# A state-space convolution with a mixture of experts on one core: x copied to the output ahead, the shared expert's sums added by transfers, and three stages in one written order

## The chip, the core and the metric

The kernel runs on one core of one Trainium2 chip. The metric is device time in microseconds (us) of one launch. TensorE (PE) does the matrix products, VectorE (DVE), ScalarE (ACT) and GpSimd (POOL) the elementwise work; transfers (DMA) are issued from the queues of SyncE (SP), ACT and POOL. Each engine works through its own instructions in their order and waits on semaphores for the others.

## The reference

```python
# x: [128, 32, 512], itok: [128] lengths
K = 2 * Re(sum_n Ct[h, n] * exp(dtA[h, n] * l))         # one kernel of 512 taps for each of 32 heads
y = causal_convolution(x, K) + x * D[:, None]           # along the 512 positions
y = y * (arange(512) < itok[:, None, None])             # cut to each row's length
t = y.reshape(4096, 512)                                # tokens
scores = sigmoid(t @ gate_w.T) + bias                   # 16 experts
w, idx = top_k(scores, 4);  w = w / sum(w)
out = sum over the 4 chosen experts of  w * (silu(t @ Wg.T) * (t @ Wu.T)) @ Wd.T
out = out + (silu(t @ Sg.T) * (t @ Su.T)) @ Sd.T        # the shared expert
return x + out.reshape(x.shape)
```

All of it is in float32. The inner size of an expert is 256.

## The kernel before

The work has three stages.

**Convolution** (loop at L831 over `NB` = 8 blocks of `HB` = 4 heads). For each head, `convolve` multiplies x (transposed on the host, `xt`) with a strip of shifted kernels (L520), masks by length into `yb` (L527, DVE), turns it with TensorE into the order by length (L530), and ACT copies it into `yT` (L531), which stays in SBUF (inside the tile `store`). Two buffers each hold `xt` and `strip`, so the loads of the next block (L151, L419, SP's queue) start at a block's start. The block's `yb` goes to the HBM buffer `y_rows` from ACT's queue (L841). `gates` then makes the gate scores of the block: partial products `parts` (L549), a copy `by_head` (L557, ACT), and sums over the quarters into `pg` (L560). After every second block `route` works out sigmoid, the best 4 of 16 and the weights `cw` on DVE (L582 to L615), turns `cw` back into row order on TensorE (`cw_ps`, L618), copies it (L620, ACT) and stores it beside the rows of `y_rows` (L621, SP).

**Shared expert** (`unit_step`, L953). The tokens are cut into `NU` = 8 units of 512. For a unit, `up` makes gate and up products (L904, `p_g` and `p_u`, each for two halves `it` of the inner size; between 1 and 4 row tiles are used, by the longest row in the unit), ACT applies Silu (L963), DVE multiplies (L966, tile `z`), and `down` makes four products of 128 tokens for the unit before (L930, two PSUM buffers `o`). The rows of x belonging to those tokens have been fetched by an indirect transfer from POOL's queue (`fetch`, L918, six buffers `xg`); DVE adds x to the product (L937), and an indirect transfer on POOL's queue puts the rows into `out` (L939). Between these pieces `next(making)` runs the next piece of the generator `slots` (L629): it counts tokens for each expert, places them in tiles of 128 slots, and builds the lists `get` and `put` with 128 pairs of one-hot matrices (L793, L794 on DVE; L782 on PE, eight in a step). The experts' weights are loaded into a ring of 8 places as their places come free (L980).

**Routed experts** (L1102 onward). For each tile of 128 slots: gather rows of `y_rows` (L869, POOL), transpose (L1012), gate and up products (L1044), Silu, multiplication with the weight, transpose (L1062), down product (L1070), copy (L1079, DVE) and an indirect transfer that adds the rows to `out` (L1080). Its output buffers are the first three of `xg`. `order` (L1092) makes SP wait for all adds so far where a new expert starts, and a tile's add waits for SP's mark.

Order: the convolution stage with `gates` and `route` is ordered by a scheduler. The units and the routed tiles are each written within `tc.manual_schedule(engines=None)` (L982 and L1102), with the rest of `making` in between. In the build, unit 0's first two up products stand ahead of the last block's `parts`, sums and `cw_ps` on PE, and the first routed transposes stand inside unit 7.

Of the kernel before, what the change touches and what calls it, by code (L numbers as in the profile page):

```python
# [31 lines left out]
I32 = mybir.dt.int32  # L32
# [43 lines left out]
def ssm_moe_kernel(  # L76
# [68 lines left out]
    y_rows = d1.tile([B * H, YW], F32, tag="y_rows", name="y_rows")  # L145
    y_bh = y_rows.rearrange("(b h) w -> b h w", h=H)
    x_rows = x.rearrange("b h l -> (b h) l")
# [117 lines left out]
    def exp_into(dst, v, name):  # L265
        shape = list(v.shape)
        k, q = (ks1.tile(shape, F32, tag=f"exp_{t}", name=f"{name}_{t}") for t in "kq")
        s = ks1.tile(shape, I32, tag="exp_s", name=f"{name}_s")
        exp_parts(v, q, k, s)
        nc.vector.scalar_tensor_tensor(dst, q, 1.0, s.bitcast(F32), ALU.add, ALU.mult)  # L270
# [10 lines left out]
    exp_into(dn.rearrange("p a c -> p (a c)"), logs.rearrange("p a c -> p (a c)"), "dn")  # L281
# [233 lines left out]
    def convolve(tb, q, xt, yb):  # L515
        h = tb * HB + q
        py = ps_g.tile([P, L], F32, tag="g", name=f"py{h}")
        for jt in range(KT):

            nc.tensor.matmul(  # L520
                py[:, : L - jt * P],
                lhsT=xt[:, jt, q, :],
                rhs=strip[tb][:, q, jt * P :],
                start=(jt == 0),
                stop=(jt == KT - 1),
            )
        nc.vector.tensor_mul(yb[:, q, :L], py, within)  # L527
        pt = ps_u.tile([P, KT, P], F32, tag="u", name=f"pt{h}")
        for kt in range(KT):
            nc.tensor.transpose(pt[:, kt, :], yb[:, q, kt * P : (kt + 1) * P], to_rank)  # L530
        nc.scalar.copy(  # L531
            yT[:, :, :, h, :].rearrange("p u k b -> p k u b"),
            pt.rearrange("p k (u b) -> p k u b", u=NU),
        )
# [5 lines left out]
    pgs = {}  # L540

    def gates(tb):


        if tb % RB == 0:
            pgs[tb // RB] = ps_o.tile([P, 512], F32, tag="o", name=f"pg{tb}")
        parts = ps_m.tile([P, NU, HB, UB], F32, tag="m", name=f"parts{tb}")
        for kt in range(KT):
            nc.tensor.matmul(  # L549
                parts[kt * QC : (kt + 1) * QC],  # L550
                lhsT=gw[:, kt, :],
                rhs=yT[:, :, kt, tb * HB : (tb + 1) * HB, :],
                start=True,
                stop=True,
            )
        by_head = yp.tile([P, HB, NU, UB], F32, tag="by_head", name=f"by_head{tb}")
        nc.scalar.copy(by_head.rearrange("p h u b -> p u h b"), parts)  # L557
        for q in range(HB):
            n = (tb * HB + q) % (RB * HB)
            nc.tensor.matmul(  # L560
                pgs[tb // RB][:, n * E : (n + 1) * E],
                lhsT=by_head[:, q].rearrange("p u b -> p (u b)"),
                rhs=gather_q,
                start=True,
                stop=True,
            )

    def route(rb):
# [14 lines left out]
        exp_into(neg, neg, f"sig{rb}")  # L583
# [31 lines left out]
        nc.vector.tensor_mul(cw, s, over_e(free))  # L615

        cw_ps = ps_m.tile([P, nh * E], F32, tag="m", name=f"cw_ps{rb}")
        nc.tensor.matmul(cw_ps, lhsT=to_row, rhs=flat(cw), start=True, stop=True)  # L618
        cw_o = stile("cw_o")
        nc.scalar.copy(flat(cw_o), cw_ps)  # L620
        nc.sync.dma_start(out=y_bh[:, hs, L:], in_=cw_o)  # L621
# [203 lines left out]


    xb = load_xt(0)
    nc.sync.dma_start(out=w_sh, in_=w_all[E])

    chunk_at = {0: CHUNKS[1], 2: CHUNKS[2], HB + 1: CHUNKS[3]}  # L830
    for tb in range(NB):  # L831
        yb = yp.tile([P, HB, L], F32, tag="yb", name=f"yb{tb}")
        x_next = load_xt(tb + 1) if tb + 1 < NB else None
        for q in range(HB):
            convolve(tb, q, xb, yb)
            if tb * HB + q in chunk_at:
                c0, n = chunk_at[tb * HB + q]
                kernels(c0, n, *waves(c0, n, 0)[0])
            if q == 0 and tb + 1 < NB:
                kernel_strip(tb + 1)  # L840
        nc.scalar.dma_start(out=y_bh[:, tb * HB : (tb + 1) * HB, :L], in_=yb)  # L841
        gates(tb)
        if tb % RB == RB - 1:
            route(tb // RB)
        xb = x_next
# [4 lines left out]

    def dep(of, on, why):
        tc.add_manual_dep(of.ins, on.ins.name, SYNC, reason=why)
# [40 lines left out]
    xg = homes(fp, "xg", [P, L], 6)  # L893
# [20 lines left out]
    def rows_of(u, q):  # L914
        return bass.IndirectOffsetOnAxis(ap=unit_rows[:, u, q : q + 1], axis=0)

    def fetch(u, q):
        nc.gpsimd.indirect_dma_start(  # L918
            out=at(xg, u * (TU // P) + q),
            out_offset=None,  # L920
            in_=x_rows,
            in_offset=rows_of(u, q),
        )

    def down(u, q):
        n = u * (TU // P) + q
        po, xq = at(p_o, n), at(xg, n)
        for it in range(IT):
# [8 lines left out]
        nc.vector.tensor_add(xq, po, xq)  # L937
        nc.gpsimd.nop()
        put = nc.gpsimd.indirect_dma_start(  # L939
            out=out, out_offset=rows_of(u, q), in_=xq, in_offset=None  # L940
        )
        for other in adds:
            tc.declare_no_dep(put.ins, other.ins, reason="other rows")
        adds.append(put)
# [8 lines left out]
    def unit_step(u):  # L953
# [3 lines left out]
        if u < NU:  # L957
            fetch(u, 0)
            fetch(u, 1)
            k_us[u] = nc.tensor.value_load(k_u[0:1, u : u + 1], min_val=1, max_val=KT)  # L960
            for it in range(IT):
                up(u, it, p_g, 0)
                nc.scalar.activation(sgu[it], p_g[it], AF.Silu)  # L963
                next(making, None)
                up(u, it, p_u, I)
                nc.vector.tensor_mul(at(zu, u)[:, it, :], sgu[it], p_u[it])  # L966
                next(making, None)
        if u > 0:
            for q in range(TU // P):
                down(u - 1, q)  # L970
        if u < NU:
            fetch(u, 2)
            fetch(u, 3)
# [7 lines left out]

    with tc.manual_schedule(engines=None):  # L982
        for u in range(NU + 1):
            unit_step(u)
    for _ in making:
        pass
    put, texp, woff, load, loff, lexp, ntk, fresh, full = (
        made[t] for t in "put texp woff load loff lexp ntk fresh full".split()
    )
# [10 lines left out]
    obs = xg[:3]  # L1000
# [5 lines left out]
    def tokens(t):  # L1006
# [9 lines left out]
        else:  # L1016
# [5 lines left out]
            texp[:, t : t + 1],  # L1022
# [11 lines left out]
    def registers(t):  # L1034
        w0s[t] = nc.tensor.value_load(
            woff[0:1, t : t + 1], min_val=0, max_val=(R - 1) * WSZ
        )
        k_ts[t] = nc.tensor.value_load(ntk[0:1, t : t + 1], min_val=1, max_val=KT)
# [28 lines left out]
    def outer(t):  # L1067
        po = at(p_o, t)
        for it in range(IT):
# [12 lines left out]
            out_offset=bass.IndirectOffsetOnAxis(ap=put[:, t : t + 1], axis=0),  # L1082
# [9 lines left out]
    def order(t):  # L1092


        new = nc.sync.value_load(fresh[0:1, t : t + 1], min_val=0, max_val=1)
# [6 lines left out]
    with tc.manual_schedule(engines=None):  # L1102
        registers(0)

        def turn_of(step):
# [15 lines left out]
            if 1 <= step < NT:  # L1121

                t = step - 1
                e = nc.sync.value_load(lexp[0:1, t : t + 1], min_val=0, max_val=E - 1)
                to = nc.sync.value_load(loff[0:1, t : t + 1], min_val=0, max_val=(R - 1) * WSZ)
                go = nc.sync.value_load(load[0:1, t : t + 1], min_val=0, max_val=1)
# [5 lines left out]
        for step in range(NT_MIN + 2):  # L1132
            turn_of(step)

        def rest(step):

            if step == NT + 2:
                return
            _, (some,) = nc.values_load_multi_w_load_instructions(
                full[0:1, step - 2 : step - 1], min_val=0, max_val=1  # L1140
# [57 lines left out]
```

## Time and profile before

| what | value |
|---|---|
| median of 3 runs | 957.14 us (956.81 to 957.47) |
| the profiled execution's own time | 961.51 us |
| its span | 959.8 us |
| TensorE busy | 890.6 us, 93% |
| VectorE, GpSimd, ScalarE busy | 427.6, 432.0, 171.3 us |
| mean granted TensorE clock | 0.985 |
| convolution ends, first unit product (L904) starts | 140.16 us |
| first routed down product (L1070) starts | 329.36 us |
| POOL: 32 fetches of x (L918), mean | 970 ns |
| POOL: 32 puts of rows (L939), mean | 984 ns |
| POOL: 134 adding transfers (L1080), mean | 1583 ns |
| DVE: 32 additions of x (L937), mean | 688 ns |

A line of the timeline gives start, length, engine, line, operation, output<-input, shapes and count, and in brackets the idle time ahead of it with the instruction that ended it. In the page's slices each digit is a tenth of busy time in 1/40 of the span. Lines of code such as L904 are those of the kernel before unless "new" stands with them.

### The profile page before, as it was taken

The numbers are of one execution on the slowest core, as the hardware profiler recorded it, in microseconds if no ns is written. First come the engines' busy times: TensorE is split into PE (matmuls) and PEld (weight loads), VectorE is DVE, ScalarE is ACT, GpSimd is POOL, SyncE is SP. The second block draws the span as 40 slices with busy tenths as digits, with TensorE's granted clock in tenths as the row PEclk, the third lists the DMA queues.
The fourth block names the chain that finished last, engine by engine and source line by source line (L and its number), as shares of the span: only waits on it lengthen the run. The fifth ranks groups of instructions, "written<-read, shape, count | busy, mean of one in ns | idle before, by whom it ended". The sixth has DMA issues, their size and how long they took to land.

```text
span 959.8 us, 14544 instructions
## 1 busy us (share of the span) xinstructions
PE 890.6 (93%) x2960; PEld 443.3 (46%) x2960; DVE 427.6 (45%) x1438; ACT 171.3 (18%) x343; POOL 432.0 (45%) x400
## 2 busy tenths in 40 slices
PE   0799994989998999999999999999999999999995
PEld 0455652344444444444444444444444544444442
DVE  7955555868762233443334233423433323334332
ACT  1122221000001012221222122212222112222211
POOL 4210002033456545664556455655555445556644
PEclk9999997989999999999999999999999999999998
DMA  4467732164456676687667766766666646677755
GB/s 161 126 228 265 233 125 68 66 223 151 165 193 196 251 166 111 127 138 164 113 119 140 166 109 120 137 108 106 125 121 114 112 90 113 112 119 138 131 110 104
DMA packets 54032, 135.94 MB, mean 142 GB/s; under 512 B 12784, under 2 KB 12944, under 8 KB 51344
## 3 DMA queue, kind: packets, MB, share of 16 engines
q0 software_dynamic: 35616, 89.77, 47.5%
q1 hardware_dynamic: 14064, 36.15, 11.4%
q10 hardware_dynamic: 4224, 8.39, 2.3%
q8 instruction: 71, 1.16, 0.5%
q14 instruction: 57, 0.47, 0.1%
HBM read 288.08 MB, written 52.25 MB: 355 GB/s over the span
## 4 chain that ended last, share of the span: by engine, by line
PE 78%; DVE 15%; issue 3%; another core or an unknown queue 1%; DMA 1%; POOL 1%; ACT 0%; SPq 0%; DVEq 0%; POOLq 0%; ACTq 0%
PE g L1044 33%; PE o L1070 24%; PE m L1012 4%; PE o L930 3%; PE u L1062 3%; PE py L520 3%; PE u L904 2%; DVE cols L794 2%; PE g L904 2%; DVE rows L793 1%; DVE yb L527 1%; PE pt L530 1%; DVE wq L261 1%; PE parts L549 1%
## 5 line engine op out<-in xcount | busy, mean ns | idle before, releaser
L1044 PE MATMUL g<-store,yt 128*128 x742 | 343.1, 596 | 4.1 <-ACT yt L1018 2.7
L1080 POOL DMA_INDIRECT out<-xg,put x134 | 212.1, 1583 | 236.5 <-DVE junk L1019 203.2
L1070 PE MATMUL o<-store,zT 128*128 x536 | 252.2, 593 | 1.3 <-DVE zT L1065 1.3
L1056 DVE SCALAR_TENSOR_TENSOR zt<-g,wt,sgt 128x256 f32<-128x256 f32 x135 | 65.3, 483 | 287.0 <-ACT sgt L1055 272.6
L1044 PEld LDWEIGHTS g<-store,yt 128*128 128x128 f32 x742 | 130.3, 190 | 121.0 <-issue 116.8
L1070 PEld LDWEIGHTS o<-store,zT 128*128 128x128 f32 x536 | 101.3, 190 | 130.5 <-issue 124.3
L869 POOL DMA_INDIRECT yg<-y_rows,get x140 | 138.8, 991 | 42.8 <-issue 30.2
L1079 DVE COPY xg<-o 128x512 f32<-128x512 f32 x134 | 92.7, 692 | 110.3 <-PE o L1070 109.4
L1018 ACT COPY yt<-m 128x512 f32<-128x512 f32 x136 | 79.6, 586 | 238.1 <-PE m L1012 225.9
L1055 ACT ACTIVATE sgt<-g 128x256 f32<-128x256 f32 x135 | 51.9, 384 | 268.6 <-PE g L1044 227.8
L1012 PEld LDWEIGHTS m<-ident,yg 128*128 128x128 f32 x373 | 48.5, 141 | 73.2 <-issue 73.0
L520 PE MATMUL py<-strip,xt 128*128 128x512 f32 (+3 forms) x256 | 77.7, 443 | 5.0 <-DMA strip<-kd 5.0
L918 POOL DMA_INDIRECT xg<-in_x,unit_rows x32 | 31.1, 970 | 108.9 <-DVE sig_k L255 99.5
L939 POOL DMA_INDIRECT out<-xg,unit_rows x32 | 31.5, 984 | 98.6 <-DVE xg L937 90.4
L930 PE MATMUL o<-store,z 128*128 128x512 f32 x128 | 60.5, 622 | 6.1 <-DVE xg L937 6.1
L1012 PE MATMUL m<-ident,yg 128*128 128x128 f32 x373 | 63.3, 273 | 1.1 <-issue 1.1
L1065 DVE COPY zT<-u 128x256 f32<-128x256 f32 x134 | 56.3, 420 | 0.1
L520 PEld LDWEIGHTS py<-strip,xt 128*128 128x128 f32 x256 | 41.9, 194 | 21.8 <-issue 9.3
L1062 PE MATMUL u<-ident,zt 128*128 128x128 f32 x268 | 51.2, 273 | 0.0
L904 PE MATMUL g<-store 128*128 128x512 f32 x92 | 44.5, 621 | 0.7 <-ACT store L531 0.7
L904 PE MATMUL u<-store 128*128 128x512 f32 x92 | 42.9, 601 | 0.8 <-issue 0.8
L930 PEld LDWEIGHTS o<-store,z 128*128 128x128 f32 x128 | 24.8, 199 | 38.0 <-issue 28.0
(272 smaller groups left out, 519.7 us busy)
## 6 DMA issues: line engine op xcount, KB each, us to landing
store<-in_w_all SPq DMA_DIRECT2D x143, 1536.0 KB
xt<-in_x_t SPq DMA_DIRECT2D x8, 1024.0 KB
y_rows<-yb ACTq DMA_DIRECT2D x8, 1024.0 KB
strip<-kd SPq DMA_DIRECT2D x7, 1024.0 KB
yg<-y_rows,get POOLq DMA_INDIRECT x140
out<-xg,put POOLq DMA_INDIRECT x134
strip<-kd SPq DMA_DIRECT2D x4, 256.0 KB
xg<-in_x,unit_rows POOLq DMA_INDIRECT x32
```

What stands on the lines that cost most here:

```text
L520: nc.tensor.matmul(py[:, : L - jt * P], lhsT=xt[:, jt, q, :], rhs=strip[tb][:, q, jt * P :], start=(jt == 0), stop=(jt == KT - 1),)
L869: nc.gpsimd.indirect_dma_start(out=at(yg, t), out_offset=None, in_=y_rows[:, :], in_offset=bass.IndirectOffsetOnAxis(ap=made["get"][:, t : ...
L904: nc.tensor.matmul(ps[it], lhsT=w_sh[:, c0 : c0 + P], rhs=yT[:, u, kt, :, :].rearrange("p h b -> p (h b)"), start=(kt == KT - n), stop=(kt ...
L930: nc.tensor.matmul(po, lhsT=at(zu, u)[:, it, q * P : (q + 1) * P], rhs=w_sh[:, c0 : c0 + L], start=(it == 0), stop=(it == IT - 1),)
L1012: nc.tensor.transpose(pt[:, q, :], at(yg, t)[:, q * P : (q + 1) * P], ident)
L1018: nc.scalar.copy(at(yt, t), pt)
L1044: mm = nc.tensor.matmul(pgu, lhsT=at(yt, t)[:, q, :], rhs=ring_flat[:, bass.ds(w0s[t] + q * 2 * I, 2 * I)], start=(q == KT - n), stop=(q = ...
L1056: nc.vector.scalar_tensor_tensor(at(zs, t), pgu[:, I:], at(wts, t), sg, ALU.mult, ALU.mult)
L1062: nc.tensor.transpose(at(p_z, t)[:, it, :], at(zs, t)[:, it * P : (it + 1) * P], ident)
L1070: mm = nc.tensor.matmul(po, lhsT=at(zts, t)[:, it, :], rhs=ring_flat[:, bass.ds(w0s[t] + WD + it * L, L)], start=(it == 0), stop=(it == IT ...
L1079: nc.vector.tensor_copy(ob, po)
L1080: add = nc.gpsimd.indirect_dma_start(out=out, out_offset=bass.IndirectOffsetOnAxis(ap=put[:, t : t + 1], axis=0), in_=ob, in_offset=None, ...
```

## The change

Four things are changed together.

1. The whole of x is copied to `out` by plain transfers within HBM on POOL's queue, one for each block's heads. Copies 0 to 3 are issued at the ends of blocks 2 to 5, copies 4 and 5 at the end of block 6, 6 and 7 at the end of block 7, each behind ACT's last copy of that block (L531).
2. In `down`, fetch, addition and put are gone: ACT copies the product into one of five buffers `ob`, and an indirect transfer on POOL's queue adds it to `out`. The routed stage uses the same five buffers.
3. `gates` is cut in two: partial products with their copy, and `sums`; `route` loses its end to `weights_out` (`cw_ps`, copy, store). For the last block, `sums` and `route` come after unit 0's first up product, and `weights_out` after unit 0's last one. The last `pg` lies in the PSUM pool `ps_m`, and the temporaries of `route` and the last `by_head` in a pool that outlives the convolution.
4. Units 0 to 7, the rest of `making` and the routed tiles are within one `manual_schedule`. The pieces of `making` are taken behind each multiplication of a unit (in unit 0 only behind the second) and behind each second down product. The last unit's down products stand after the first routed tile's transposes and before the second tile's.

```diff
+    COPIES = {2: (0,), 3: (1,), 4: (2,), 5: (3,), 6: (4, 5), 7: (6, 7)}
...
         for q in range(HB):
-            convolve(tb, q, xb, yb)
+            turned = convolve(tb, q, xb, yb)
...
         nc.scalar.dma_start(out=y_bh[:, tb * HB : (tb + 1) * HB, :L], in_=yb)
+        for part in COPIES.get(tb, ()):
+            own = slice(part * HB, (part + 1) * HB)
+            x_out = nc.gpsimd.dma_start(out=out_bh[:, own, :], in_=x[:, own, :])
+            dep(x_out, turned, "behind the block")
         gates(tb)
-        if tb % RB == RB - 1:
-            route(tb // RB)
+        if tb + 1 < NB:
+            sums(tb)
+            if tb % RB == RB - 1:
+                route(tb // RB)
+                weights_out(tb // RB)
...
-    xg = homes(fp, "xg", [P, L], 6)
+    obs = homes(fp, "ob", [P, L], 5)
...
     def down(u, q):
...
-        nc.vector.tensor_add(xq, po, xq)
+        nc.scalar.copy(ob, po)
         nc.gpsimd.nop()
-        put = nc.gpsimd.indirect_dma_start(
-            out=out, out_offset=rows_of(u, q), in_=xq, in_offset=None
+        add = nc.gpsimd.indirect_dma_start(
+            out=out,
+            out_offset=bass.IndirectOffsetOnAxis(ap=unit_rows[:, u, q : q + 1], axis=0),
+            in_=ob,
+            in_offset=None,
+            compute_op=ALU.add,
         )
...
         if u < NU:
-            fetch(u, 0)
-            fetch(u, 1)
             k_us[u] = nc.tensor.value_load(k_u[0:1, u : u + 1], min_val=1, max_val=KT)
             for it in range(IT):
                 up(u, it, p_g, 0)
+                if u == 0 and it == 0:
+                    sums(NB - 1)
+                    route(NB // RB - 1)
                 nc.scalar.activation(sgu[it], p_g[it], AF.Silu)
-                next(making, None)
                 up(u, it, p_u, I)
                 nc.vector.tensor_mul(at(zu, u)[:, it, :], sgu[it], p_u[it])
-                next(making, None)
-        if u > 0:
-            for q in range(TU // P):
+                if u > 0 or it > 0:
+                    next(making, None)
+        if u == 0:
+            weights_out(NB // RB - 1)
+        for q in range(TU // P):
+            if u > 0:
                 down(u - 1, q)
-        if u < NU:
-            fetch(u, 2)
-            fetch(u, 3)
+                if q % 2 == 1:
+                    next(making, None)
...
-    with tc.manual_schedule(engines=None):
-        for u in range(NU + 1):
-            unit_step(u)
-    for _ in making:
-        pass
...
-    obs = xg[:3]
...
     with tc.manual_schedule(engines=None):
+        dep(nc.tensor.nop(), parts_last[0], "in TensorE's order")
+        for u in range(NU):
+            unit_step(u)
+        for _ in making:
+            pass
         registers(0)
...
-        for step in range(NT_MIN + 2):
+        turn_of(0)
+        unit_step(NU)
+        for step in range(1, NT_MIN + 2):
             turn_of(step)
```

## The prediction

> **What bounds the kernel now.** I read the page first: shares, slices, chain. TensorE (PE) is busy 93% of the span, and the chain of work that ended last lies 78% on it.
>
> ```profile
> PE   0799994989998999999999999999999999999995
> PEclk9999997989999999999999999999999999999998
> PE 78%; DVE 15%; issue 3%; another core or an unknown queue 1%; DMA 1%; POOL 1%; ACT 0%; SPq 0%; DVEq 0%; POOLq 0%; ACTq 0%
> ```
>
> A slice is 24 us. After the start-up PE sags only in slices 7 and 9 (144 to 168, 192 to 216 us), and there its clock sags too. So the routed stage, 331 to 945 us, is solid PE work that the change leaves alone; time can only move between 50 and 331 us. There I read PE's timeline. Columns: start, length, engine, line, operation; in brackets the idle time before it and who ended it.
>
> ```profile
> 140.16 3.70 PE L904 MATMUL g<-store 128*128 128x512 f32 x8 [0.67 <-ACT store L531]
> ...
> 149.74 0.37 PE L560 MATMUL pg<-gather_q,by_head 128*128 128x16 f32 x2
> 162.03 0.80 PE L618 MATMUL cw_ps<-cw,to_row 128*128 128x128 f32 x2 [11.92 <-DVE cw L615]
> ...
> 162.87 5.60 PE L904 MATMUL g<-store 128*128 128x512 f32 x8
> ...
> 183.42 3.60 PE L904 MATMUL u<-store 128*128 128x512 f32 x8
> 186.85 3.60 PE L930 MATMUL o<-store,z 128*128 128x512 f32 x8
> 194.76 6.72 PE L930 MATMUL o<-store,z 128*128 128x512 f32 x8 [4.31 <-DVE xg L937]
> 201.31 2.74 PE L904 MATMUL g<-store 128*128 128x512 f32 x6
> ...
> 219.02 3.70 PE L930 MATMUL o<-store,z 128*128 128x512 f32 x8 [0.58 <-DVE xg L937]
> 222.56 2.74 PE L904 MATMUL g<-store 128*128 128x512 f32 x6
> ...
> 329.36 1.13 PE L1070 MATMUL o<-store,zT 128*128 x2 [1.29 <-DVE zT L1065]
> ```
>
> The reader is to see two stalls (11.92 and 4.31 us), each followed by a group that takes nearly twice its usual time (5.60 and 6.72 against 3.60), and a unit that comes round every 21.2 us (201.31 to 222.56). VectorE's (DVE's) timeline fills the first stall: from 150.16 to 161.98 it works through the last routing, `neg` to `cw`. Then the DMA shares in one convolution block (columns: stretch, busy us of each engine, clock, DMA share, GB/s):
>
> ```profile
> 59.00:63.00 4.00, 3.97 (x19) 2.36 (x18) 0.92 (x2) 0.75 (x2) 0.00 (x0) 1.00 0.85 247
> 63.00:69.00 6.00, 6.00 (x35) 3.71 (x34) 2.53 (x10) 1.60 (x3) 0.00 (x0) 1.00 0.96 346
> 69.00:71.50 2.50, 2.46 (x13) 1.54 (x12) 2.29 (x8) 0.59 (x1) 0.00 (x0) 1.00 0.10 39
> ```
>
> A block of 13.2 us moves 3 MB (next x, next strip, y out); the transfers are full for 10 us and free for some 2.5.
>
> **What the Trainium skill says.** "TensorE: Matmul & The Clock Gate", section "What's actually happening": after an idle window of about 3.4 us the array falls to half rate until it has been busy as long. The trace agrees: both groups behind the stalls are slow, while the group after the 2.66 us stall at 310.84 takes its usual 3.70. "DMA: Bandwidth & Descriptors", "Issuing engines are not separate DMA queues": GpSimd's transfers use the same 16 engines as SP's and ACT's. So the copy of x isn't free for being on an idle queue; the trace agrees in that two queues share at about half each from 64 to 68 us. Same page, "Anatomy of one DMA": bytes / 436e3 us, an estimate of 2.4 us for 1 MB; no row of before shows HBM-to-HBM copies.
>
> **The change, part by part.** Prices for full-clock PE work come from the timeline's start-to-start times: an up group 3.43, 2.57 or 1.72 us (4, 3 or 2 row tiles), a pair of down products 3.43, eight one-hot products (L782) 0.50.
>
> *Units 0 and 1* took 140.16 to 201.31, 61.2 us. Their work is 8 ups x 3.43 = 27.5, 4 downs 6.9, gate parts and sums 1.9, `cw_ps` and the small planning products 1.6: 37.9. So 23.3 us are lost: 11.9 + 2.0 (5.60 less 3.60) + 4.3 + 3.1 (6.72 less 3.60) and 2.0 in small waits. In the new order the last sums follow the first up group, and three more ups (10.3 us) stand ahead of `cw_ps`. Sums end near 140.2 + 1.0 + 3.4 + 0.9 = 145.5; routing without the two steps that had slipped in (0.69 `z`, 0.86 counting) is 10.3 us, so `cw` is there at 156; PE arrives at 155.8. I leave 1.0 us. Queued behind `cw_ps` on PE is unit 1; nothing on SP but the gate store. The 4.31 us wait goes since `o` is emptied by ACT (0.59 us a copy, L531), which has 3.6 us of work in a unit of 16 to 22. Before, DVE put one-hot work (3.1 us from 190.91) ahead of the emptying. What is late next: slots' long DVE chain (11 + 5 us) runs to about 193, ahead of unit 2's first `z`, which unit 3's PE work needs at about 200. Covered.
>
> *Units 2 to 5* start at 201.31, 222.56, 243.72, 264.89 and end at 283.11: 81.8 us. Work: 3 x (4 x 2.57 + 6.87 + 2.0) + (4 x 1.72 + 6.87 + 2.0) = 73.2. Lost 8.6. DVE loses 4 x 0.69 us a unit and has 12.4 + 1.4 = 13.8 us left, against 15.8 to 19.2 on PE; one-hot steps move behind `z` and behind each pair of downs, 3.8 us of DVE against 3.9 of PE. I leave 1.5 us of small waits.
>
> *Units 6, 7 and the routed start*, 283.11 to the first L1070 pair done at 331.3: 48.2 us, work 43.8. The fetch of x that held DVE (5.5 us at 327.66) is gone. I leave 1.0 us for the routed stage's own filling. The gathers come from the end of unit 6, one unit (13.7 us) ahead of their use, behind four adds on GpSimd's (POOL's) queue (4 x 1.9 = 7.6 us): covered.
>
> Lost in all 36.3 us, of which 1.0 + 1.5 + 1.0 stay: gain 32.8.
>
> *The adds.* 32 fetches (0.97 us) and 32 puts (0.98) on POOL, 62 us, become 32 adds at L1080's 1.58, 51 us. On the engines: in 380 to 420 us the software queue moves about 9.2 gathers and adds in 27.3 us of full share; a gather at the fetch's rate (0.93 MB in 3.2 us) is 0.94, so an add is 2.0 us. A unit's four take 8 us of DMA in 14 to 20 us; a buffer of five comes back after five downs, over 7 us at the tightest place (down of unit 7 right behind that of 6). I take nothing; bounds 0 and 5. Below nothing is excluded: PE has no idle time left there that isn't counted above. The last adds hold the routed stage's first add through SP's wait; they land about 10 us ahead of it.
>
> *The copy.* Parts 0 to 3 leave POOL at the ends of blocks 2 to 5, beside x, strip and y of the next block; parts 4 to 7 meet no load. POOL is idle there (its timeline shows nothing from 51.6 to 151 us). Each adds 1 MB to 10 us of full transfers. At the busy stretch's 346 GB/s it is 3.0 us, 0.5 more than the free 2.5; strip then lands late and PE waits. Bounds: 2.4 us (the skill's estimate): nothing; the add's 2.0 us per 0.26 MB, 7.7 us a MB: 5.2 late. Four blocks: 0 to 21 us, not below 0, since no load becomes earlier. I take 0.75 each, 3.0, a little over the nearest row because reads and writes both fall on HBM.
>
> **Sum.** -32.8 + 3.0 = -29.8, rounded to -29 for waits that I don't see. The profiled execution took 961.51 us, 1.7 more than its span of 959.8; the three runs lie at 957.14 in the median. The difference carries over: 957.1 - 29 = 928.
>
> **Rivals.**
> 1. *The copies stall the convolution, in part.* For: transfers are 96% full for six of 13 us. Against: 2.5 us are free in each block. At 7.7 us a MB 21 us come back: -12, 945.
> 2. *The written order makes a new wait.* DVE and ACT are in order; ACT's first Silu now waits for all earlier SP and ACT transfers, with the copies beside them, and five add buffers may come back late. Against: the spare times above. About 10 us lost: 938.
> 3. *Slower: the copy itself is slow.* Same place as 1; it decides from (32.8 / 4) + 2.5 = 10.7 us a MB. At 12.5 us a MB: 4 x 10.0 - 32.8 = +7, 964. For: nothing shows this operation. Against: the slowest row of the software queue gives 7.7.
> 4. *The order does not take hold*, PE still waits out the routing: about the same time, 957. Against: the build's instruction list has the sums behind the first up group and `cw_ps` behind the fourth.
>
> **Chances.** Forecast (921 to 933) 0.69; rival 1 0.11; rival 2 0.12; rival 3 0.05; rival 4 0.03. The range is the forecast's span and most of rival 2: 921 to 941. Rivals 1 and 2 and the forecast are faster by over 0.2% (about what a measurement of this kernel tells from no change): 0.92. Rival 4 gives 0.02 to no change and 0.01 to slower, rival 3 is slower: same 0.02, slower 0.06.
>
> **What would show it.** Right: PE's clock line without a dip after slice 2; `cw_ps` waits under 2 us; up groups of 3.4 to 3.6 us right behind it; units 2 to 4 in 18 to 20 us; the first L1070 near 301 us. Wrong: PE waiting for strip or xt at the block starts near 85, 98, 112 and 125 us by more than 2 us each (copy mis-sized); `ob` waiting for its add; Silu waiting for DMA; or a routed stage that is no longer solid.

## The result and the profile after

| | median, us | lowest to highest |
|---|---|---|
| before (4 runs) | 956.97 | 956.22 to 957.47 |
| after (4 runs) | 942.95 | 941.50 to 944.60 |

The ratio is 0.9855, 95% interval 0.9836 to 0.9873. The change gains 14.0 us. The forecast was 29 (928.0, range 921 to 941), so the sign was right, the size twice too large, and the time lies just above the range. The profiled execution of the changed kernel took 942.44 us, its span is 940.7.

The page of the changed kernel, in the lines that the prediction showed of before (slices of 23.5 us, then the shares of the chain that ended last):

```profile
PE   0799997999999999999999999999999999999993
PEclk9999999999999999999999999999999999999997
PE 66%; issue 1%; SPq 0%; POOL 0%; DVE 0%; ACT 0%; POOLq 0%
```

Counted from 1, as in the prediction, slice 7 holds a 7 where it held a 4, slice 9 a 9, and the dips of the clock are gone. (Slice 10 holds a 7 too; the timeline shows no wait there, and the second and third profiles have a 9.) The shares of the chain can't be set against those of before: this chain reaches back to 290.1 us only, and its shares add to 67%. In the third profile it reaches the start, and DVE has 10% of it against 15%. The last slice holds a 3 where there was a 5. TensorE's timeline of the changed kernel (start, length, engine, line, operation, idle time before and who ended it):

```profile
85.66 1.10 PE L520 MATMUL py<-strip,xt 128*128 128x512 f32 x2 [0.21 <-DMA strip<-kd]
100.00 1.10 PE L520 MATMUL py<-strip,xt 128*128 128x512 f32 x2 [1.21 <-DMA strip<-kd]
127.97 1.10 PE L520 MATMUL py<-strip,xt 128*128 128x512 f32 x2 [1.46 <-DMA strip<-kd]
...
143.56 1.06 PE L551 MATMUL parts<-store,gw 128*32 128x512 f32 x8 [0.68 <-ACT store L531]
146.31 3.69 PE L929 MATMUL g<-store 128*128 128x512 f32 x8 [1.68 <-issue]
...
162.28 0.46 PE L631 MATMUL cw_ps<-cw,to_row 128*128 128x128 f32 x2 [1.09 <-DVE cw L623]
163.26 3.69 PE L929 MATMUL g<-store 128*128 128x512 f32 x8 [0.52 <-ACT cw_o L635]
...
204.65 2.84 PE L929 MATMUL g<-store 128*128 128x512 f32 x6 [0.87 <-issue]
...
290.58 7.10 PE L944 MATMUL o<-store,z 128*128 128x512 f32 x16 [1.18 <-ACT yt L1028]
...
305.81 1.88 PE L1080 MATMUL o<-store,zT 128*128 x4
...
924.45 1.88 PE L1080 MATMUL o<-store,zT 128*128 x4
```

The 11.92 us wait for `cw` is 1.09; the group behind it takes 3.69 and not 5.60; the 4.31 us wait for DVE to empty `o` is gone. New are three short waits for strip (2.9 us), 1.68 us ahead of the first up group that the timeline puts down to nothing (`issue`), 0.87 us of the same kind in unit 3, and 1.18 us for `yt`. The first routed down product starts at 305.81, 23.6 us before that of the kernel before (329.36). Most of the signs that the prediction named for being right are there: no dip in the clock line, `cw_ps` waiting under 2 us, units 2 to 4 in 19.1 to 19.6 us, no wait for strip above 2 us. Only the first routed down product, forecast near 301, comes later.

And the DMA shares in one convolution block (stretch, busy us of each engine with the numbers of instructions, clock, DMA share, GB/s):

```profile
77.00:83.00 6.00, 5.89 (x32) 3.07 (x30) 3.54 (x12) 1.78 (x4) 0.00 (x0) 1.00 1.00 380
83.00:85.50 2.50, 2.45 (x16) 1.94 (x16) 0.01 (x1) 0.59 (x1) 0.00 (x0) 1.00 1.05 335
```

The 2.5 us of a block in which the transfers were nearly free are full now, as the prediction had it.

The last routed down product starts at 924.45; in the kernel before it starts at 947.72. So the lead is still 23.3 us when the last product runs, yet the spans differ by 19.1. The other 4.1 us are lost behind the last product: it ends at 926.33 and the span at 940.7, 14.3 us later; before it was 949.60 and 959.8, 10.2. A group of instructions by line has the reason. The columns are line, engine queue, operation, count, shortest/median/longest in ns, first and last start. After, then before (its second profiled execution):

```profile
L1212 POOLq DRAIN  x3: 46/109/5623, 934.2 to 940.4; - x3
```

```profile
L1194 POOLq DRAIN  x3: 46/107/2195, 951.8 to 954.6; - x3
```

The longest of GpSimd's closing drains takes 5.62 us after and 2.20 before (2.20 in its first profile too). The page doesn't count a drain as busy time.

### The profile page after: what moved, and what is told of

It reads as the page before. It is cut to its first block, busy times and chain, and to the rows that moved or that the text cites. A ratio compares the mean times of both kernels' runs of the same rounds, so it can differ in the third digit from the quotient of the medians.

```text
span 940.7 us, 14509 instructions
## 1 busy us (share of the span) xinstructions
PE 883.1 (94%) x2960; PEld 442.0 (47%) x2960; DVE 409.3 (44%) x1406; ACT 190.0 (20%) x375; POOL 422.7 (45%) x376
## 3 DMA queue, kind: packets, MB, share of 16 engines
q1 hardware_dynamic: 14064, 36.15, 11.3%
## 4 chain that ended last, share of the span: by engine, by line
PE 66%; issue 1%; SPq 0%; POOL 0%; DVE 0%; ACT 0%; POOLq 0%
PE g L1054 34%; PE o L1080 24%; PE m L1022 4%; PE u L1072 3%; PE o L944 1%; POOL out L1090 0%; SPq L1157 0%; POOL yg L894 0%; SPq L1105 0%; SPq L1140 0%; SPq L1141 0%; DVE zt L1066 0%; SPq L1142 0%; ACT sgt L1065 0%; SPq L880 0%
## 5 line engine op out<-in xcount | busy, mean ns | idle before, releaser
L1090 POOL DMA_INDIRECT out<-ob,put x134 | 211.3, 1577 | 242.6 <-DVE junk L1029 214.4
L1066 DVE SCALAR_TENSOR_TENSOR zt<-g,wt,sgt 128x256 f32<-128x256 f32 x135 | 65.3, 484 | 306.7 <-ACT sgt L1065 306.7
L1089 DVE COPY ob<-o 128x512 f32<-128x512 f32 x134 | 92.7, 692 | 109.7 <-PE o L1080 101.6
L953 POOL DMA_INDIRECT out<-ob,unit_rows x32 | 50.2, 1568 | 98.8 <-ACT ob L951 93.1
L944 PE MATMUL o<-store,z 128*128 128x512 f32 x128 | 57.7, 597 | 1.2 <-ACT yt L1028 1.2
L865 POOL DMA_DIRECT2D out<-in_x x8 | 4.4, 558 | 88.3 <-ACT store L531 88.3
L809 DVE TENSOR_SCALAR cols<-tpos_h,stl,tok 128x143 f16<-128x143 f16 x128 | 41.8, 331 | 0.0
```

The lines of the kernel that those rows point to most:

```text
L944: nc.tensor.matmul(po, lhsT=at(zu, u)[:, it, q * P : (q + 1) * P], rhs=w_sh[:, c0 : c0 + L], start=(it == 0), stop=(it == IT - 1),)
L1066: nc.vector.scalar_tensor_tensor(at(zs, t), pgu[:, I:], at(wts, t), sg, ALU.mult, ALU.mult)
L1089: nc.vector.tensor_copy(ob, po)
L1090: add = nc.gpsimd.indirect_dma_start(out=out, out_offset=bass.IndirectOffsetOnAxis(ap=made["put"][:, t : t + 1], axis=0), in_=ob, in_offse ...
```

## The experiments

The theory at the outset, A: the mechanisms were right, and the missing 15 us are a sum of small things: the profiled execution that I counted in wasn't typical of the plain runs (some 5 us), the tail behind the last product (4), and unforeseen waits at unit starts (5). The main rival, C: the copies and the adding transfers cost most of it, by taking DMA time all over.

**1. Both kernels again, and each half of the change alone.** Four kernels on one chip.

> The kernel before once more, with a second profiled execution. My theory A: some 5 us of the missing 15 were never in the plain runs: the first profiled execution (961.5) was 4.4 us above its plain median, by chance of that one execution, so part of the 36.3 us of losses that I added up belonged to it alone. A expects a plain median of 957 and a profiled span of 954 to 957 this time, with the slow groups behind the two stalls shorter or the tail shorter. Rival B: profiled executions of this kernel are always longer than plain ones by 4 to 5 us; then the span is again 959 to 960 and the losses are the same to 0.5 us.

Measured (before_again): 956.9 us, and a profiled execution of 956.57 with a span of 954.9, against 961.51 and 959.8 the first time. A's numbers came. But the difference isn't in the slow groups, it is at the routed start: the first L1070 starts at 324.82 and not at 329.36. ScalarE's timeline around it, first execution, then the second:

```profile
299.14 0.60 ACT L963 ACTIVATE sg<-g 128x512 f32<-128x512 f32 x1 [10.09 <-PE m L1012]
309.71 0.60 ACT L963 ACTIVATE sg<-g 128x512 f32<-128x512 f32 x1 [9.97 <-remote]
```

```profile
298.09 0.60 ACT L963 ACTIVATE sg<-g 128x512 f32<-128x512 f32 x1 [9.70 <-PE g L904]
301.64 0.60 ACT L963 ACTIVATE sg<-g 128x512 f32<-128x512 f32 x1 [2.95 <-PE g L904]
```

In the first execution the second Silu of unit 7 comes 8 us later than in the second, although PE had written its input by 302.3; "remote" means that the profile names nobody who let it go. DVE stands still with it (10.59 us ahead of 308.33). In the second execution neither does. The chain that ended last in the first execution goes through this standstill:

```profile
299.17 10.57 another core or an unknown queue
```

That is the "another core or an unknown queue 1%" of the chain line which the prediction shows, and slice 13 there (288 to 312 us) holds an 8. In the second profile the chain has no such share, and the slice a 9.

> The changed kernel once more. Plain median 942 to 943 against the kernel before at 957. The stretch from the end of the last product of the routed stage (L1080) to the end of the span was 14.3 us against 10.2 before. Theory A: that tail belongs to the program, so it is again 13.5 to 15 us. Rival B: it is chance of one execution, and this time it lies anywhere between 10 and 14 us, with the plain times unchanged.

Measured (after_again): 943.55 us (ratio 0.9857, 0.9842 to 0.9872). The tail is again 14.3 us (925.51 + 1.88 to 941.7), the drain again 5.62. It belongs to the program.

> The written order alone: x is fetched, added by VectorE and put as before, no copies. Five xg buffers in place of six, so that three of the four fetches of a unit come behind the products of the unit before it. Theory A (the copies cost the 3 us that I gave them, the adds nothing): the conv stage gains back 2.9 us, but VectorE empties the shared outputs again and waits for fetches, some 5 to 8 us in units 1 to 7, so 943 to 948. Rival C (the copies and adds cost most of the missing 15 us, by sharing the DMA engines all over): the order alone gives 930 to 935.

```diff
-    COPIES = {2: (0,), 3: (1,), 4: (2,), 5: (3,), 6: (4, 5), 7: (6, 7)}
-        for part in COPIES.get(tb, ()):
...
-        nc.scalar.copy(ob, po)
+        nc.vector.tensor_add(xq, po, xq)
...
-            compute_op=ALU.add,
```

Measured (order_alone): 948.05 us, ratio 0.9902 (0.9886 to 0.9917), at the upper end of A's range. TensorE's waits from 60 to 320 us (engine, tile, line, who: us in total, times, longest):

```profile
PE o L949 <- DVE xg L956: 5.9, 3, 3.1
PE g L923 <- issue: 4.5, 5, 1.6
PE cw_ps L631 <- DVE cw L623: 1.3, 1, 1.3
```

The routing stall is gone by the order alone; the wait for DVE to add x into `o` stays.

> The copies and the adding transfers alone: the order is the scheduler's as before, the routing stall of some 12 us stays. Theory A: 957 less 4.3 and 3.1 (the wait for xg and the slow group behind it) less some 4 in units 2 to 7, plus 3 for the copies: 946 to 951. Rival C (copies and adds cost some 15 us): 955 to 962.

```diff
+        for part in COPIES.get(tb, ()):
+            own = slice(part * HB, (part + 1) * HB)
+            x_out = nc.gpsimd.dma_start(out=out_bh[:, own, :], in_=x[:, own, :])
...
-        nc.vector.tensor_add(xq, po, xq)
+        nc.scalar.copy(ob, po)
```

Measured (copies_alone): 955.74 us, ratio 0.9987 (0.9980 to 0.9994): C's number, not A's. The waits, again from 60 us on:

```profile
PE cw_ps L618 <- DVE cw L615: 11.8, 1, 11.8
PE py L520 <- DMA strip<-kd: 2.8, 2, 1.5
```

So the copies cost 2.8 us and the stall stays, as A said, and the last routed product starts 4.7 us before that of the second profile of before (938.41 against 943.10). Then the tail takes it back: 14.4 us against 9.9. C is refuted: the order alone came to 948 and not to 930 to 935, and here the costs are in named places. A's price was too low for two reasons: it had left out the tail, and from unit 2 to the routed start the kernel gains some 2 us on the second profile of before, where A had 4. The halves alone gain 8.9 and 1.2 us, both in one kernel 14.0: each alone leaves a stall that the other takes away.

**2. One suspected cost at a time in the changed kernel.** Four kernels on one chip, before at 956.76 us.

> The changed kernel with all eight copies of x issued behind the last block of the convolution, where no strip, x or y transfer is left. Theory A: the three waits for strip at block starts (2.9 us) go, the tail behind the last product stays at 14.3 us, so 939.5 to 941.5 against 943. The first adds of the shared stage start near 176 us and eight copies of about 3.3 us (26 us) end near 170, so they don't hold. Rival D (the adds then wait for the copies, the five ob buffers fill up and TensorE waits in units 1 and 2): 943 to 950.

```diff
-    COPIES = {2: (0,), 3: (1,), 4: (2,), 5: (3,), 6: (4, 5), 7: (6, 7)}
+    COPIES = {7: (0, 1, 2, 3, 4, 5, 6, 7)}
```

Measured (copies_late): 939.77 us, ratio 0.9818 (0.9805 to 0.9831). No wait for strip is left, the first routed product starts at 302.56 (3.2 us earlier), the tail is 14.6. The copies fill the DMA engines from 143 to about 170 us; the adds begin at 177 and hold nothing. D is out.

> The changed kernel with the copies of x issued by ScalarE's queue at the same places, in place of GpSimd's. Both profiles of the changed kernel and that of the copies alone end in a drain on GpSimd of 5.62 us, the kernels without copies in one of 2.19, and the last semaphore step on GpSimd takes 1.53 against 0.68. Theory E: it is the copies as plain transfers on GpSimd's own queue that lengthen the end, so here the tail is 10 us and the time 938 to 940, with the strip waits of 2.9 us unchanged. Rival F: it is the 32 adding transfers that lengthen it, so the tail stays at 14.3 us and the time at 942 to 944. ScalarE's first Silu may wait for the last copies; TensorE does not need it before 163 us.

```diff
-            x_out = nc.gpsimd.dma_start(out=out_bh[:, own, :], in_=x[:, own, :])
+            x_out = nc.scalar.dma_start(out=out_bh[:, own, :], in_=x[:, own, :])
```

Measured (copies_on_act): 939.1 us, ratio 0.9814 (0.9799 to 0.9828). The time is what E expected and the reason is not: the tail is 13.8 us, and the drain still long.

```profile
L1212 POOLq DRAIN  x3: 46/107/4971, 931.1 to 936.6; - x3
```

What went instead are the waits for strip: none from 60 us on. The copies and their bytes are the same, and a copy now stands in the queue behind the block's `yb`. But the run changes a second thing. The scheduler, which orders the convolution, built another order: TensorE's products there come in the same sequence in the kernel before, the changed kernel, copies_alone and copies_late, and in another one here. This order is itself shorter. The last block's gate products start 1.7 us earlier than in copies_late, which has no copies in the convolution at all (copies_late, then copies_on_act):

```profile
140.59 1.06 PE L551 MATMUL parts<-store,gw 128*32 128x512 f32 x8 [0.68 <-ACT store L531]
```

```profile
138.94 1.07 PE L551 MATMUL parts<-store,gw 128*32 128x512 f32 x8 [0.67 <-ACT store L531]
```

So whether the waits for strip went because of the queue, because of the place behind `yb` or because of the new order isn't shown. The Trainium skill, "DMA: Bandwidth & Descriptors", section "SWDGE vs HWDGE vs iDMA", advises this queue: "transpose or plain → SP/ACT (HWDGE)", and only accumulating, casting or irregular transfers to GpSimd. The time agrees, by 3.9 us (939.1 against the 943 of the changed kernel), but no run here shows the queue to be the reason, and with all copies late GpSimd's queue comes within 0.7 us (939.77).

> The changed kernel with the register of unit 0 (the number of its row tiles) loaded ahead of the convolution, as in the kernel before, in place of behind the gate products. Theory A: the 1.68 us in which TensorE waits for nothing shown ahead of the first up group is this load; it goes and 0.1 us stays, but VectorE's routing starts as much earlier only in part (it starts behind the last sums), so the wait for cw grows by nothing: 941 to 942 against 943. Rival G: the wait is the first fetch of the shared stage's instructions, and moves nothing: 943.

```diff
+    k_us = {0: nc.tensor.value_load(k_u[0:1, 0:1], min_val=1, max_val=KT)}
     xb = load_xt(0)
```

Measured (ku_early): 940.99 us, ratio 0.9835 (0.9822 to 0.9849), 2.0 us less than the changed kernel; G is out. The load is in the trace: by line and queue, with count, shortest/median/longest ns, first and last start, in the kernel before and in the changed one:

```profile
L960 PEldq TENSOR_LOAD <-k_u x8: 297/307/484, 15.1 to 294.4; - x8
```

```profile
L976 PEldq TENSOR_LOAD <-k_u x8: 297/318/793, 144.8 to 271.9; - x8
```

With it at the start again, the wait of 1.68 is 0.34:

```profile
144.94 3.69 PE L930 MATMUL g<-store 128*128 128x512 f32 x8 [0.34 <-PE parts L551]
```

The load was worth more than the 1.34 us that went there. In the third profile of the changed kernel (as in the second) the group behind this wait is slow, with a granted clock of 0.60 from 146 to 150 us:

```profile
146.40 5.39 PE L929 MATMUL g<-store 128*128 128x512 f32 x8 [1.65 <-issue]
```

In the first profile it took 3.69, at a clock of 1.00. The skill page that the prediction used, "TensorE: Matmul & The Clock Gate", section "What's actually happening", has the half rate follow an idle window of about 3.4 us. Here no wait is that long: 0.9, 0.7 and 1.7 us lie within 5 us, and the clock falls in some executions and not in others. That is a likely reason why the changed kernel's own runs spread over 3 us and those with the early load over 1.2; it isn't shown, and copies_late, with the late load, spreads over 1.6.

> The changed kernel with the shared sums put in place of added (x is left out of the output of the tokens). It prices the 32 adding transfers: theory A says they cost nothing on the path, so 942 to 944 and the same tail of 14.3 us. Rival F (the adds lengthen the end): tail 10 us and 938 to 940. Rival C (the adds take DMA time from the routed start): the first product of the routed outputs 1 us or more earlier.

```diff
-            compute_op=ALU.add,
```

(in `down` alone.) Measured (puts_for_adds): 941.08 us, ratio 0.9833 (0.9819 to 0.9846), some 2 us less than the adds and 1 us under A's range. The products from the first to the last routed one take 618.0 us against 618.6, and the first starts at 305.67 against 305.81: on the path the adds cost nothing that can be told from chance, as forecast. The tail is 13.2 us in place of the 14.3 that A had, the drain 4.81 in place of 5.62. F is right in the small and wrong as the reason of the tail: 0.8 of the 3.4 us by which the drain grew.

**3. What sets the closing drain, and what the waits are worth together.** By now neither the copies on GpSimd nor the adds explained the drain. What was left is their number. Counted by the page's groups, GpSimd issues 134 + 140 + 32 + 32 = 338 transfers before, and 134 + 140 + 32 + 8 = 314 after.

> The changed kernel with 24 small fetches more on GpSimd (128 rows of 64 bytes each, never used), in time in which GpSimd is idle, so that it issues 338 transfers, as in the kernel before, and not 314. GpSimd's closing drain took 2.19 us with 338 transfers (both kernels with fetches and puts), 5.62 with 314, 4.97 with 306 and 4.81 with 314 of which 32 put in place of adding. Theory H: the drain clears what is left of the transfers' bookkeeping at the end, and depends on how many were issued in all, rising with the number and falling back from time to time; so this drain differs from 5.62 by over 0.5 us, and the number 338 may bring it to 2 to 3 us, the time to 939 to 941. Rival I: it belongs to the kinds of transfers used, and stays at 5.6, the time at 943 or, where the fetches hold up a strip, 944.

```diff
+            for i in range(24 if tb * HB + q == HB + 1 else 0):
+                pad = nc.gpsimd.indirect_dma_start(
+                    out=pads[i % 8],
+                    out_offset=None,
+                    in_=x_bits,
+                    in_offset=bass.IndirectOffsetOnAxis(ap=unit_rows[:, i // 4, i % 4 : i % 4 + 1], axis=0),
+                )
```

```profile
L1223 POOLq DRAIN  x3: 46/109/3016, 955.3 to 958.8; - x3
```

In this run (pad24) the drain is 3.02 us: H, and I is out. Behind the last product lie 11.2 us in place of 14.3. The whole time, 961.25 us, says nothing of it: while GpSimd issued the 24 fetches one behind another, the other engines stood still, as ScalarE's timeline shows.

```profile
66.15 0.58 ACT L563 COPY by_head<-parts 128x512 f32<-128x512 f32 x1 [2.28 <-PE py L520]
86.55 0.58 ACT L531 COPY store<-pt 128x512 f32<-128x512 f32 x1 [19.82 <-remote]
```

PE lost 15.9 us to that ahead of 89.45 us, on the chip on which the kernel before took 961.16.

> The same with 8 small fetches more (322 transfers). Theory H: if the drain rises by some 0.1 us a transfer as from 306 to 314, 6.3 us here, or it falls back to under 5. Rival I: 5.6 us.

```profile
L1223 POOLq DRAIN  x3: 46/109/6195, 934.8 to 941.5; - x3
```

6.20 us (pad8) where 6.3 was expected. The whole time is 945.02 us, on the same chip as pad24 (ratio 0.9832, 0.9817 to 0.9847).

> The changed kernel with the waits found taken out together: copies by ScalarE's queue (no waits for strip, 3 us), the registers of row tiles each loaded one step earlier (1.7 and 0.9 us, and no slow group behind the first), the gate weights sent out in unit 1 in place of behind unit 0 (1.1 + 0.5 us), the first turning of gathered tokens between the last products (1.2 us). Theory: 942.9 - 3.0 - 2.6 - 1.6 - 1.2 - 0.5 for the end, so 934. If these waits only move to the next step (rival J), 937 to 939, as with the copies alone moved.

```diff
+            if u + 1 < NU:
+                k_us[u + 1] = nc.tensor.value_load(k_u[0:1, u + 1 : u + 2], min_val=1, max_val=KT)
...
-        if u == 0:
-            weights_out(NB // RB - 1)
+                if u == 1 and it == 0:
+                    weights_out(NB // RB - 1)
...
                 down(u - 1, q)
+                if u == NU and q == 0:
+                    turn_of(0)
```

(with the copies on ScalarE's queue and the first register loaded early, as above.) Measured (best_act): 932.38 us against 961.16 for the kernel before on that chip, ratio 0.9701 (0.9688 to 0.9715). J is out: the waits don't come back elsewhere. It is 1.6 us better than the sum; the convolution has the shorter order of copies_on_act, which the sum left out.

> The same with all copies by GpSimd's queue behind the last block. Theory: 934 to 935 (the end 0.5 us longer than with the copies on ScalarE's queue). If the adds wait for the copies now that the units begin 2 us earlier, 936 or more.

Measured (best_late): 934.83 us, ratio 0.9724 (0.9710 to 0.9737), drain 5.62: within its range, but 2.4 us above best_act, where 0.5 were expected. The convolution has the old order again and ends 1.7 us later (140.62 against 138.96); the stretch behind the last product is 0.6 us longer.

**4. What was still open.** Whether the first execution's 4.6 us belong to a chip, and whether the end can be shortened by the number of transfers alone. Four kernels on one chip.

> The kernel before, a third profiled execution. Theory K (a chip has its own level): where the plain runs are at 957, the first L1070 pair starts near 324.8 us and the span is 955; where they are at 961, it starts near 329.4 and VectorE and ScalarE stand still for some 8 us from 300 us on. Rival L (chance of an execution): start and level don't go together.

Measured (before_third): 956.76 us, span 955.0, first L1070 at 324.60. This chip is at 957, so only one half of K was tried, and it holds.

> The changed kernel on the same chip. Theory K: it has no such stall on any chip, so 942 to 945 wherever it runs, and the gain is 14 us on a chip with the kernel before at 957 and 16 to 19 us on one with 961.

Measured (after_third): 943.13 us, ratio 0.9856 (0.9841 to 0.9871). The changed kernel wasn't run on a chip at 961. Of the nearest to it, pad8 took 945.02 there, with 8 idle fetches and a drain 0.6 us longer. The level of that chip is thus one of the kernel before: best_act took 932.38 there and, as the next run shows, 932.49 here.

> The version with the waits taken out and the copies by ScalarE's queue again: 932 to 933, end of the last product to end of span 13.8 us with a drain of 4.97.

Measured (best_act_2): 932.49 us, ratio 0.9754 (0.9741 to 0.9767), with 13.5 us behind the last product. The longest waits of PE from 60 to 310 us:

```profile
PE parts L551 <- ACT store L531: 0.7, 1, 0.7
PE u L1076 <- DVE zt L1070: 0.6, 1, 0.6
PE g L930 <- PE parts L551: 0.3, 1, 0.3
```

> The same with 30 small fetches more on GpSimd, five in each of six blocks of the convolution (336 transfers in all). Theory H (the drain follows the number of transfers, and falls back between 322 and 338): the drain is 2.5 to 3.3 us, the semaphore step 0.9, so 2.2 to 2.8 us less, 929.5 to 931. Rival M (what falls back depends on where in the run the transfers come): drain 5.5 to 8 us, 933 to 936. If the fetches hold up strips, TensorE waits at block starts and the drain alone counts.

```diff
+            for i in range(5 * tb - 5, 5 * tb) if q == 1 and 1 <= tb <= 6 else ():
+                pad = nc.gpsimd.indirect_dma_start(
```

```profile
L1226 POOLq DRAIN  x3: 46/107/2843, 923.8 to 927.2; - x3
```

Measured (best_pad30): 929.86 us, ratio 0.9722 (0.9709 to 0.9735), 2.6 us less than best_act_2 beside it. The last product starts at 914.91 against 914.74, so the whole gain lies behind it. Five at a time, the fetches hold nobody up. M is out. The drains together:

| kernel | transfers on GpSimd | drain, us |
|---|---|---|
| copies_on_act, best_act | 306 | 4.97 |
| after, copies_alone, copies_late, ku_early, best_late | 314 | 5.62 |
| pad8 | 322 | 6.20 |
| best_pad30 | 336 | 2.84 |
| pad24 | 338 | 3.02 |
| before, order_alone | 338 (32 fetches and 32 puts, no copies, no unit adds) | 2.20, 2.19 |
| puts_for_adds | 314 (32 puts in place of adds) | 4.81 |

It rises by 0.07 to 0.09 us a transfer and falls back somewhere between 322 and 336; a unit's add counts 0.025 us more than a put (0.81 / 32). The same 0.82 us stand between pad24 and the kernel before, both with 338: the one has 32 unit adds, the other 32 puts. The bytes don't matter: eight copies of 1 MB add 0.65 us, eight fetches of 8 KB 0.57. Every indirect transfer here moves 128 rows, so whether the transfers count or their rows isn't told apart. What is cleared up there the profile doesn't show.

## Why the prediction was wrong

By its own steps, in the first profiled executions of both kernels (before at 961.51, after at 942.44):

| step | forecast gain, us | measured gain, us |
|---|---|---|
| copy, to the end of the convolution | -3.0 | -3.4 |
| units 0 and 1 (140.16 to 201.31; now 143.56 to 185.53) | 22.3 | 19.2 |
| units 2 to 5, with unit 6, into which one-hot work slid (201.31 to 296.84; now 185.53 to 275.06) | 7.1 | 6.0 |
| unit 7 to the first routed down products done (to 331.3; now to 307.5) | 3.4 | 2.0 |
| routed stage to its last product | 0 | -0.3 |
| behind the last product | 0 | -4.1 |
| from the profiled executions to the plain medians | 0 | -4.9 |

The forecast column adds to 29.8, the measured one to 14.5; the medians (957.14 and 942.95) differ by 14.2, and the rest lies in the cutting points. So three steps failed. "The difference carries over" cost 4.9 us, "time can only move between 50 and 331 us" 4.1, and the waits left for the units and the routed start, 3.5 us in the prediction, were 5.6 too small (3.1 + 1.1 + 1.4).

*The convolution.* Right: 2.9 us of waits for strip, in three of the four blocks, against 3.0; the rest is 0.45 us that the trace is later at 22 us already.

*Units 0 and 1.* Right in mechanism: the stall of 11.9, both slow groups and the 4.3 us wait went. "I leave 1.0 us" was too little: PE loses 1.68 to the load of `k_u` with its branches, 1.09 to `cw`, and 0.52 that the profile puts down to the copy of `cw` (the register load of unit 1 stands in the same place, at 162.3 us). One term failed in the list of what is moved: in the kernel before the register load of unit 0 stood at the program's start (15.1 us), put there by the scheduler, and the written order sets it behind the last `parts` (144.8 us). It is one line of the built order, and it moves with the step; I costed matrix products and DVE work only. ku_early gives it 2.0 us. The other is the routing, "10.3 us": it takes 11.3 (150.84 to 162.14 on DVE). Taking out the two steps that had slipped in saved 0.5 us of the 11.8 it took before, and not their full 1.55. That is the wait for `cw`.

*Units 2 to 5.* Nearly right: 0.87 of the missing 1.1 us stands behind the register load of unit 3, and goes where the registers are loaded a step earlier (best_act).

*Unit 7 and the routed start.* The gathers were early enough, as said. But unit 7's down products now stand behind the first tile's transposes, and by the profile PE waits 1.18 us there for ACT's copy of these to `yt`. With the transposes between the down products (best_act) the wait is gone. I had looked at how much work ACT has in a unit (3.6 us for the emptying), and not at what PE would wait for behind that turn. The 2.0 us gained are all of the standstill in the first execution: against the second profile of before, where this stretch takes 30.5 us (296.18 to 326.70), the 32.4 us of the changed kernel are a loss of 1.9.

*The adds.* Right: nothing on the path.

*Behind the last product.* "Time can only move between 50 and 331 us" is the step that was plainly wrong. The kernel has fewer GpSimd transfers, which I had booked as a saving of 11 us beside other work; on the closing drain it costs 3.4 us (0.8 of them for adds in place of puts, the rest with the number), and 0.85 on GpSimd's semaphore step ahead of it (1.53 against 0.68). The tail of 10.2 us was there in the profile of before, and I took it for fixed.

*"The difference carries over."* Wrong by 4.9 us, 4.4 of them in the kernel before. The sum was made against an execution of 961.51, whose routed start held a standstill of some 8 us on two engines, worth 4.5 us of the end, which the plain runs at 957.1 did not have. I had booked its 2.66 and 1.29 us of waits as losses that the change removes; in the second profile they are 0.24 and none. Seventeen plain runs of the kernel before on one chip took 961.16 in the median, on the three others 956.4 to 957.0; so it looks like a level that this kernel has on a chip, but no profile of the kernel before was taken on that one, and this stays open.

*The rivals.* Rival 1 named a time near the measured one (945) for the wrong reason: the copies cost 2.9 us, not 21. Rival 2, new waits in the written order, is what happened in the units, at 4.3 us (1.68 + 0.87 + 1.18 + 0.6 beyond what I had left for `cw`) and not 10. Rivals 3 and 4 did not occur.

With the waits taken out, another order in the convolution and the drain short, the kernel runs in 929.9 us, 26.5 us under before. So most of the forecast gain was there to be had, though in part in places that the prediction did not count.

## What to carry to other kernels

When a step moves from a scheduler's order into a written one, list its register loads with its products: one load of a loop count with its branches, 1.7 us on TensorE, cost as much as an up group of two row tiles (1.72). Before a profiled execution is used as the base of a sum, take its own time against the plain runs; where it is 4 us longer, find those 4 us first and strike them from the losses. And cost the end of the program too: the time from the last product to the end of the span is no constant. Where a scheduler orders a stage, a change of one queue can bring another order with it: compare the sequences before the gain is put down to the queue.

## What the runs showed of the hardware that was not expected

- GpSimd's closing drain depends on how many transfers it has issued: 4.97, 5.62, 6.20 us for 306, 314, 322, and 2.84 and 3.02 for 336 and 338. 32 adds in place of puts are 0.8 us of it. Thirty useless fetches made a kernel 2.6 us faster.
- Copies of x from GpSimd's queue beside the loads of strip held TensorE up by 2.9 us. From ScalarE's queue there was no such wait, but the convolution had another order there, so the queue isn't shown to be the reason.
- 24 small fetches one behind another on GpSimd (0.95 us each) went with a standstill of the other engines of up to 19.8 us, while the DMA engines were 10% busy or less (from 72 us on); eight in a row or five in a row did not. The cause is not settled. The standstill in the first profile of before looks alike, with GpSimd issuing eighteen transfers in a row (284.3 to 306.7); but the second profile has such a row too, and no standstill.
